# Scan stage of a Mamba, MoE and latent-attention kernel issued in its written order, with loads by their use and the first half's experts and feed-forwards in one queue

## The chip, the cores and the metric

The kernel runs on one core of a Trainium2 chip. The metric is the device time of one launch in microseconds. Three runs of the kernel before took 973.04 to 975.01 us, with a median of 973.29 us. Engines are named as in the profile: PE (matrix products), DVE (vector), ACT (scalar), POOL (GpSimd), SP (issues most of the transfers).

## The reference

Four sequences of 512 tokens and 128 channels pass through three blocks with residuals, and the second kind of block is used twice:

```python
x = x + mamba_then_moe(layernorm(x))
x = x + ffn(layernorm(x))
x = x + latent_attention(layernorm(x))
x = x + ffn(layernorm(x))

def mamba_then_moe(x):
    h = rmsnorm(x, rms1_w)
    xi, z = split(h @ in_proj_w, 2)              # 256 channels each
    xi = silu(causal_conv(xi, conv_w) + conv_b)  # 4 taps
    dt, Bm, Cm = split(xi @ x_proj_w)            # 64, 16, 16
    delta = softplus(dt @ dt_proj_w + dt_proj_b)
    A = -exp(A_log)
    for t in tokens:                             # 16 states per channel
        h_t = exp(delta_t * A) * h_t + (delta_t * xi_t) * B_t
        y_t = sum over states of h_t * C_t
    y = (y + D_skip * xi) * silu(z)
    h = x + y @ out_proj_w
    m = rmsnorm(h, rms2_w)
    top2 of softmax(m @ router_w) over 8 experts
    return h + sum over top2 of weight * (silu(m @ Wg[e]) * (m @ Wu[e])) @ Wd[e]

def latent_attention(x):                         # 16 heads of 8, 64 latents
    q_lat = per head (x @ W_dq.T @ W_uq.T) @ k_eff
    c_kv = x @ W_dkv.T
    return causal softmax(q_lat @ c_kv.T / sqrt(8)) @ c_kv @ v_eff

def ffn(x):                                      # integer weights times 1/127
    return (silu(x @ wg.T) * (x @ wu.T)) @ wd.T
```

## The kernel before

All 512 tokens of a sequence lie on the free axis during the scan: channels are two halves of 128 partitions, so that a tile is 128 x 1024. One state of one sequence is a *step*; there are 4 x 16 = 64 steps, counted by s, in the loop at L733. A step (`scan`, L635) issues:

- `decay(s+2)`, L607: ACT makes the decays da of two steps later, and SP loads the row of C, cs, over all partitions.
- bx, L646: DVE multiplies delta times xi (du) with the row of B that `spread` (L618) put over the partitions with a PE product, pb.
- hst, L650: DVE's scan along the tokens.
- hc, L655: POOL multiplies with cs.
- `accumulate`, L626: PE adds the hc of the step before into PSUM (yp).

Beside these the loop advances generators, a piece at each step. `front(b+1)` (L519) makes the projections, the convolution and delta of the next sequence. `close(b-1)` (L664) ends the one before: y, output projection, RMS norm, router logits, `route` (L698, top two) and `number` (L226, rows of the tokens in the list sorted by expert). `scatter` (L263) writes the tokens to their rows in DRAM, with indirect transfers on POOL. At step 7 of the third sequence `experts(0)` (L326) and two `combine` (L381) are put into the queue `work`, of which a step issues one piece. The sequences form two groups, [0, 1] and [2, 3], and `experts(g)` runs 23 tiles of 128 rows for a group, each tile with three weight loads of 256 KB on SP; tile i's transpose, tile i-1's gate and up products with tanh, and tile i-2's halving (L321) and down product stand in one piece. `plan(g)` (L276) tells which expert and which rows a tile has. `combine` gathers each token's two expert rows with indirect transfers on POOL.

The order of instructions on each engine in this stage is the scheduler's, which starts from the order in which the pieces are written.

Ahead of the loop come the moments of all four sequences (L477 on, `moments` L158, `rsqrt` L142), the integer weights (L499), the zeroing of the two sorted lists xg as two transfers of 4 MB, and three small products that make w_up and veff.

The last stage (L761 on) is the attention with both feed-forwards. `project(b)` (L824) makes queries and keys, each as a sum of three bf16 parts (`three`, L815), and stores them (q_d, k_d) to DRAM; `fill(u)` (L864) loads them for a unit of 8 heads. `maxima(u)` (L875) finds each row's maximum, which goes back to the queries as three more rows through DRAM (m_d). `exps(G)` (L920) makes the exponentials for 4 heads (st on PE, p on ACT), `weigh(G)` (L953) the weighted sums and `divide(G)` (L969) the quotient. Units 0 to 7 run in the loop at L1045, which also steps the queue with `experts(1)`, `combine(2)`, `first_ffn(2)`, `project(2)` and so on to `last(b)`, the second feed-forward of a sequence.

Of the kernel before, what the change touches and what calls it, by code (L numbers as in the profile page):

```python
# [28 lines left out]
WBUFS = 3  # L29
PBUFS = 12  # L30
GROUPS = [[0, 1], [2, 3]]
BIG = 3.0e38


@with_exitstack
def block_kernel(ctx, tc, x, rms1_w, rms2_w, in_proj_w, conv_w, conv_b, x_proj_w,
# [8 lines left out]
    xs = []  # L45
    for b in range(B):
        xt = keep.tile([P, NT, C], F32, tag="x", name=f"x{b}")
        nc.sync.dma_start(xt, x[b].rearrange("(t p) c -> p t c", p=P))
        xs.append(xt)
# [8 lines left out]

    r1w = load("r1w", [P, 1, 1], column(rms1_w, 1), nc.scalar)
    w_in = load("w_in", [P, 2 * EI], in_proj_w, nc.scalar)  # L60
# [4 lines left out]
    A = load("A", [P, NE, NS], A_log.rearrange("(c p) n -> p c n", p=P), nc.scalar)  # L65
    Dk = load("Dk", [P, NE, 1], column(D_skip, NE), nc.scalar)
    w_op = load("w_op", [P, NE, C], out_proj_w.rearrange("(c p) m -> p c m", p=P))
    r2w = load("r2w", [P, 1, 1], column(rms2_w, 1))
    w_rt = load("w_rt", [P, NEXP], router_w)
    w_qk = const.tile([P, 2 * KVL], F32, tag="w_qk", name="w_qk")  # L70
    nc.sync.dma_start(w_qk[:, 0:KVL], W_dqT)
    nc.sync.dma_start(w_qk[:, KVL : 2 * KVL], W_dkvT)
    w_dq = load("w_dq", [KVL, C], W_dq)
    w_uq = load("w_uq", [KVL, C], W_uqT)
    w_uk = load("w_uk", [P, KVL], W_uk)
    w_uv = load("w_uv", [P, KVL], W_uv)
    w_o = load("w_o", [P, C], W_oT)
# [64 lines left out]
    def rsqrt(v, n, pool=small, tag="rs"):  # L142

        r = pool.tile([P, n], F32, tag=f"{tag}{n}", name="rs_r")
# [23 lines left out]
    def layernorm(dst, src):  # L168
        mv = moments(src)
        v = small.tile([P, NT], F32, tag="v", name="ln_v")  # L170
        nc.vector.tensor_scalar(v, mv[:, :, 1], EPS, None, ALU.add)
        r = rsqrt(v, NT)
        for t in range(NT):
            nc.vector.tensor_scalar(
                dst[:, t, :], src[:, t, :], mv[:, t, 0:1], r[:, t : t + 1], ALU.subtract, ALU.mult
            )

# [9 lines left out]
    def transposed(ps, dst, src, scale=None):  # L187

        pt = ps.tile([P, L], F32, tag="mm", name="pt")
        for t in range(NT):  # L190
            nc.tensor.transpose(pt[:, t * P : (t + 1) * P], src[:, t, :], ident)
        if scale is None:
            nc.scalar.copy(dst, pt)
        else:
            nc.scalar.activation(dst, pt, AF.Copy, scale=scale)

    hs = [keep.tile([P, NT, C], F32, tag="hs", name=f"hs{b}") for b in range(B)]
# [18 lines left out]
    ps = ctx.enter_context(tc.tile_pool(name="ps_m", bufs=1, space=PSUM))  # L216
# [9 lines left out]
    def number(b):  # L226
# [12 lines left out]
        nc.vector.tensor_copy(tot, pr[:, 1].rearrange("p j e -> p e j"))  # L239
# [14 lines left out]
        nc.vector.tensor_tensor(row, inc.rearrange("p e j -> p j e"), pr[:, 0], ALU.add)  # L254
# [71 lines left out]
    def experts(g):  # L326
# [4 lines left out]
        xT, wgu, wd, hidden = {}, {}, {}, {}  # L331
        for i in range(NTILES + 2):
            if i < NTILES:
                e = nc.sync.value_load(both[0:1, 0, i : i + 1], min_val=0, max_val=NEXP - 1)
                at = nc.sync.value_load(
                    both[0:1, 1, i : i + 1], min_val=0, max_val=NEXP * ROWS - P
                )
                xt = wt.tile([P, C], F32, tag="xt", name="xt", bufs=3)
                nc.sync.dma_start(xt, sorted_x[g][bass.ds(at, P), :])
# [3 lines left out]
                wd[i] = wt.tile([P, NFC, C], F32, tag="wd", name="wd", bufs=WBUFS)  # L343
# [3 lines left out]
            if i >= 2:  # L347
# [3 lines left out]
            if i < NTILES:  # L351
                pt = ps.tile([P, P], F32, tag="mm", name="mpt")
                nc.tensor.transpose(pt, xt, ident)
                xT[i] = wt.tile([P, P], F32, tag="xTm", name="xTm", bufs=3)
                nc.scalar.activation(xT[i], pt, AF.Copy, scale=r2w[:, 0, :])  # L355
            if 1 <= i <= NTILES:
                x, w = xT.pop(i - 1), wgu.pop(i - 1)
                pgu = []
                for k in range(2):
                    pp = ps_s.tile([P, NFC, P], F32, tag="sc", name=("mpg", "mpu")[k])  # L360
                    for f in range(NFC):
                        nc.tensor.matmul(  # L362
                            pp[:, f, :], w[:, k, f * P : (f + 1) * P], x, start=True, stop=True
                        )
                    pgu.append(pp)
                th = wt.tile([P, NFC, P], F32, tag="thm", name="thm")
                nc.scalar.activation(th, pgu[0], AF.Tanh, scale=0.5)  # L367
                hidden[i - 1] = th, *pgu
            if i >= 2:
# [6 lines left out]
                y = wt.tile([P, C], F32, tag="ym", name="ym")  # L376
                nc.scalar.copy(y, pd)
                nc.sync.dma_start(sorted_y[g][(i - 2) * P : (i - 1) * P, :], y)
            yield

    def combine(b):  # L381

        g = place[b][0]
        for t in range(NT):
            for k in range(2):
# [4 lines left out]
                )  # L390
                nc.vector.scalar_tensor_tensor(
                    base[b][:, t, :], yk, gates[b][:, t, k : k + 1], base[b][:, t, :],
                    ALU.mult, ALU.add,
                )
                yield
# [22 lines left out]
    by_head = w_up.rearrange("p (d h) -> p h d", h=NH)  # L418
    nc.vector.tensor_copy(by_head[0:KVL], w_uq.rearrange("p (h d) -> p h d", d=HS))
    pk = ps.tile([P, L], F32, tag="mm", name="pk")  # L420
    nc.tensor.matmul(pk[:, 0:C], w_uq, w_dq, start=True, stop=True)
# [704 lines left out]
```

## Time and profile before

The profiled execution took 975.5 us, and its span on the core is 973.8 us (1.7 us lie around it).

| Engine | busy us | share of the span | instructions |
|---|---|---|---|
| PE, products | 747.4 | 77% | 3588 |
| DVE | 625.7 | 64% | 1266 |
| ACT | 332.7 | 34% | 576 |
| POOL | 272.7 | 28% | 190 |

| Mark in the trace | us from the span's start |
|---|---|
| first hst | 58.2 |
| first hst of sequences 1, 2, 3 | 128.5, 225.2, 323.1 |
| last hst ends | 445.4 |
| first softmax tile (st) | 572.4 |
| ffn(2) transposes start | 710.8 |
| end | 973.8 |

Transfers moved 92.69 MB, a mean of 95 GB/s. A busy PE in the table is not PE at its peak, since the clock that the chip grants (PEclk in the page) stands at 0.853 in the mean. The span is divided by the marks into a part in which DVE has the most to do (the scan), a part in which neither DVE nor PE is full, and a part in which PE is.

### The profile page before, as it was taken

The page shows a single profiled execution, that of the slowest core. Times are in us where ns is not written, and L with a number is a line of the kernel's source. Part 1 is how long each engine was busy: PE and PEld are TensorE (multiplying, and loading weights), DVE is VectorE, ACT ScalarE, POOL GpSimd, SP SyncE. Part 2 cuts the span into 40 slices and gives each one's busy share as a digit, 9 for nine tenths or more (in the row PEclk, how much of TensorE's full clock was granted, in tenths as well). Part 3 has the DMA queues.
Part 4 walks back from the last instruction along what each step waited for, and adds up shares of the span by engine and source line. Part 5 has one row for each costly group of instructions (what it writes and reads, how often), then busy time and mean ns, then how long its engine had stood idle before and what let it go on. Part 6 is the DMA issues. An engine that isn't in the chain of part 4 may idle for free.

```text
span 973.8 us, 11231 instructions
## 1 busy us (share of the span) xinstructions
PE 747.4 (77%) x3588; PEld 407.9 (42%) x3588; DVE 625.7 (64%) x1266; ACT 332.7 (34%) x576; POOL 272.7 (28%) x190
## 2 busy tenths in 40 slices
PE   0878567766687976787266899979478999999894
PEld 0322222323234743575123366866333445444342
DVE  6279899789988899744754655542257475655523
ACT  0477322352236422321011044324311454433440
POOL 2046664476456443613620000000320010000000
PEclk9989796887699988989577589989776899989898
DMA  8612121111115752563146063855400342100000
GB/s 255 235 48 73 43 65 54 44 44 54 55 48 173 218 159 81 156 205 103 44 122 162 18 166 88 242 176 158 112 20 30 87 116 63 39 13 14 3 11 11
DMA packets 81084, 92.69 MB, mean 95 GB/s; under 512 B 9441, under 2 KB 56489, under 8 KB 79849
## 3 DMA queue, kind: packets, MB, share of 16 engines
q1 hardware_dynamic: 77105, 86.81, 30.2%
q0 software_dynamic: 2048, 4.20, 1.5%
q10 hardware_dynamic: 1872, 0.97, 0.4%
q8 instruction: 28, 0.46, 0.2%
q14 instruction: 31, 0.25, 0.1%
HBM read 70.71 MB, written 21.17 MB: 94 GB/s over the span
## 4 chain that ended last, share of the span: by engine, by line
PE 46%; DVE 27%; issue 11%; DMA 7%; ACT 5%; POOL 2%; SPq 1%; ACTq 0%; POOLq 0%; DVEq 0%
DVE hst L650 9%; PE po L960 6%; DVE bx L646 5%; PE yp L631 4%; PE sc L886 4%; PE st L937 4%; PE mpd L373 3%; PE pg L783 3%; DMA xt<-xg 3%; PE mpu L362 3%; PE mpg L362 2%; DVE mx L895 2%; PE fpd L792 2%; DMA yk<-yg,rows_y 2%; PE pm L538 2%
## 5 line engine op out<-in xcount | busy, mean ns | idle before, releaser
L631 PE MATMUL yp<-hc,ident 128*128 128x512 f32 x256 | 165.9, 755 | 69.0 <-POOL hc L655 66.8
L655 POOL TENSOR_TENSOR hc<-hst,cs 128x1024 f32<-128x1024 f32 x64 | 151.2, 2362 | 159.3 <-DVE hst L650 31.4
L650 DVE TENSOR_TENSOR_SCAN hst<-da,bx 128x1024 f32<-128x1024 f32 x64 | 145.9, 2280 | 2.8
L895 DVE TENSOR_REDUCE mx<-sc 128x1 f32<-128x512 f32 (+3 forms) x176 | 109.1, 638 | 43.0 <-PE sc L890 40.8
L611 ACT ACTIVATE da<-delta,A 128x512 f32<-128x512 f32 (+1 forms) x128 | 86.0, 713 | 141.4 <-DVE hst L650 103.1
L950 ACT ACTIVATE p<-st 128x512 f32<-128x512 f32 x160 | 90.9, 597 | 102.7 <-PE st L945 101.3
L631 PEld LDWEIGHTS yp<-hc,ident 128*128 128x128 f32 x256 | 53.6, 229 | 145.3 <-POOL hc L655 109.7
L646 DVE TENSOR_TENSOR bx<-du,pb 128x1024 f32<-128x1024 f32 x64 | 78.5, 1226 | 28.3 <-PE pb L621 24.0
L886 PE MATMUL sc<-ks,qs 72*128 72x128 bf16 (+3 forms) x256 | 71.4, 339 | 9.4 <-DVE mx L895 7.9
L960 PE MATMUL po<-p,va 128*32 128x512 f32 (+3 forms) x512 | 76.3, 447 | 0.0
L323 DVE SCALAR_TENSOR_TENSOR thm<-thm,mpg 128x512 f32<-128x512 f32 x46 | 31.4, 684 | 67.4 <-ACT thm L367 67.4
L387 POOL DMA_INDIRECT yk<-yg,rows_y x32 | 30.4, 950 | 138.5 <-DMA ks<-k_d 128.1
L937 PE MATMUL st<-qs,ks 75*128 75x512 bf16 (+3 forms) x256 | 63.8, 313 | 1.3 <-ACT p L950 0.9
L373 PE MATMUL mpd<-wd,mh 128*128 128x128 f32 x368 | 55.0, 296 | 2.7 <-ACT xTm L355 1.9
L362 PE MATMUL mpu<-xTm,wgu 128*128 128x128 f32 x368 | 53.6, 288 | 3.6 <-DVE mh L324 1.9
L373 PEld LDWEIGHTS mpd<-wd,mh 128*128 128x128 f32 x368 | 49.4, 206 | 13.9 <-ACT xTm L355 9.4
L986 POOL TENSOR_TENSOR base<-x,yn 128x512 f32<-128x512 f32 x4 | 5.1, 1267 | 177.4 <-DVE yn L981 177.4
L362 PE MATMUL mpg<-xTm,wgu 128*128 128x128 f32 x368 | 54.1, 290 | 0.6 <-DVE thm L323 0.6
L362 PEld LDWEIGHTS mpg<-xTm,wgu 128*128 128x128 f32 x368 | 50.4, 207 | 4.1 <-DVE thm L323 1.7
L362 PEld LDWEIGHTS mpu<-xTm,wgu 128*128 128x128 f32 x368 | 48.9, 204 | 7.3 <-DVE mh L324 4.5
L890 PE MATMUL sc<-maskq,identb 128*128 128x128 bf16 (+2 forms) x176 | 48.1, 273 | 0.0
L886 PEld LDWEIGHTS <-qs 72*128 72x128 bf16 x256 | 25.6, 109 | 42.0 <-issue 35.4
(229 smaller groups left out, 1079.9 us busy)
## 6 DMA issues: line engine op xcount, KB each, us to landing
cs<-c_d SPq DMA_DIRECT2D x64, 256.0 KB
wgu<-in_Wg_dram SPq DMA_DIRECT2D x46, 256.0 KB
wgu<-in_Wu_dram SPq DMA_DIRECT2D x46, 256.0 KB
wd<-in_Wd_dram SPq DMA_DIRECT2D x46, 256.0 KB
xg<-zero SPq DMA_DIRECT2D x2, 4096.0 KB
k_d<-parts SPq DMA_DIRECT2D x12, 384.0 KB
qs<-q_d SPq DMA_DIRECT2D x24, 192.0 KB
ks<-k_d SPq DMA_DIRECT2D x24, 192.0 KB
```

The lines of the kernel that those rows point to most:

```text
L362: nc.tensor.matmul(pp[:, f, :], w[:, k, f * P : (f + 1) * P], x, start=True, stop=True)
L373: nc.tensor.matmul(pd, hT[:, f, :], w[:, f, :], start=(f == 0), stop=(f == NFC - 1))
L611: nc.scalar.activation(da[:, e, e:], delta[b][:, e, e:], AF.Exp, scale=A[:, e, n : n + 1])
L631: nc.tensor.matmul(yps[b][:, e, :], ident, hc[:, e, :], start=(n == 0), stop=(n == NS - 1))
L646: nc.vector.tensor_tensor(bx, du[b], pb.unsqueeze(1).to_broadcast([P, NE, L]), ALU.mult)
L650: nc.vector.tensor_tensor_scan(hst.rearrange("p e l -> p (e l)"), dec.pop(s).rearrange("p e l -> p (e l)"), bx.rearrange("p e l -> p (e l) ...
L655: nc.gpsimd.tensor_tensor(hc, hst, cs.unsqueeze(1).to_broadcast([P, NE, L]), ALU.mult)
L886: nc.tensor.matmul(sc[:, c : c + w], q[0:NP9, h, t * P : w], k[0:NP9, h, 0:w], start=(h == h0), stop=False, skip_group_check=True,)
L895: nc.vector.tensor_reduce(mx[:, t, h0 : h0 + n], sc[:, 0 : n * w].rearrange("p (h k) -> p h k", k=w), AX.X, ALU.max,)
L937: nc.tensor.matmul(pt[:, c : c + L - kt * P], k[0 : NP9 + 3, h0 + j, rows], q[0 : NP9 + 3, h0 + j, kt * P : L], start=(c == 0), stop=False ...
L950: nc.scalar.activation(p, pt, AF.Exp, scale=scale)
L960: nc.tensor.matmul(po[32 * j : 32 * j + 32, kt * P : L], vs[b % 2][:, kt, (4 * g + j) * (HS + 1) : (4 * g + j) * (HS + 1) + 32], got[j][kt ...
```

## The change

The lines are numbered here as in the changed kernel. It does the following.

- **Order.** Everything from the moments of x0 to the last scatter is issued inside `tc.manual_schedule(engines=ORDERED)`: PE, DVE, ACT and SP keep the order in which the code is written. POOL stays with the scheduler, but `queued` ties what is written for it between two steps' products hc to that place, with dependences that carry no wait. The attention stage is left to the scheduler, and its pools take `reuse_waits="tile"`.
- **Start.** x0 and the weights of `front(0)` are loaded first, and moments and deviations are made for x0 alone. `early()` makes the others, the zeroing (8 transfers of 1 MB), the integer weights and `prepare()` (w_up, veff, constants of the values), a piece at each step of the first sequence.
- **Steps.** `front` and `close` have more and smaller pieces; `close` begins at step 1 and not 0, `scatter` at 6 and not 4 with two a step, `experts(0)` at 9 and not 7. In the last sequence every second step takes two pieces of `work`. Copies of logits, counts and of the output projection are on ACT, the sum h2 on POOL.
- **Experts.** Rows are loaded a tile ahead, results stored a tile later, and buffers of the gate and up weights are 2 and not 3.
- **Feed-forward.** `ffn` moves to the common part; its xn, xT and fh have one buffer each, shared with `project`; the end is a copy on ACT and a sum on POOL. `first_ffn(0)` and `first_ffn(1)` follow `combine(0)` and `combine(1)` in the queue, which is emptied before `project(0)`.
- **Attention.** `project`'s parts are split on POOL, which also issues the stores of q_d and k_d and both transfers of m_d. `maxima` issues a tile's reduce behind the next tile's products; `weigh` holds the quotient too; the evacuations of mT, values and quotients are on ACT. The queue is stepped by a rate (0.8, 0.7, 0.4 a piece).

```diff
-WBUFS = 3
+WBUFS = 2
+ORDERED = {ENG.PE, ENG.DVE, ENG.Activation, ENG.SP}
...
+        def early():
+            for b in range(1, B):
+                moments(xs[b], mv0[:, b])
+            yield
+            deviations(range(1, B))
+            yield
+            zero = w1.tile([P, NE * L], F32, tag="y", name="zero")
+            nc.gpsimd.memset(zero, 0.0)
...
+            yield from prepare()
...
+        order = mybir.DependencyInfo(mybir.DependencyClass.NoSync, mybir.DependencyReason.DATA)
+        mark = []
+        def queued(ins):
+            traced = nc.cur_bb.bb.instructions
+            if mark:
+                at = next(k for k in reversed(range(len(traced))) if traced[k] is mark[0])
+                between = [i for i in traced[at + 1 :] if i.engine == ENG.Pool and i is not ins]
+                for i in between:
+                    tc.add_manual_dep(i, mark[0].name, order, reason="behind the step's product")
+                for i in between or mark:
+                    tc.add_manual_dep(ins, i.name, order, reason="before the step's product")
+            mark[:] = [ins]
...
-            h2 = w2.tile([P, NT, C], F32, tag="h2", name="h2")
-            nc.vector.tensor_tensor(h2, h0[b], po, ALU.add)
+            h2 = w1.tile([P, NT, C], F32, tag="h2", name="h2")
+            nc.scalar.copy(h2, po)
+            nc.gpsimd.tensor_tensor(h2, h0[b], h2, ALU.add)
+            yield
...
+        with tc.manual_schedule(engines=ORDERED):
+            moments(xs[0], mv0[:, 0])
+            deviations([0])
...
                 for n in range(NS):
                     scan(b * NS + n)
-                if n == 0 and b:
-                    behind = close(b - 1)
-                next(behind, None)
-                if n == 4 and b:
+                    if n >= 1:
+                        next(behind, None)
+                    if n == 6 and b:
                         rows_out.add(scatter(b - 1))
-                rows_out.step(3)
+                    rows_out.step(2)
                     if n >= 2:
                         next(ahead, None)
-                if n == 7 and b and place[b - 1][1] == len(GROUPS[0]) - 1:
+                    if n == 9 and b and place[b - 1][1] == len(GROUPS[0]) - 1:
                         g = place[b - 1][0]
                         work.add(experts(g), *(combine(i) for i in GROUPS[g]))
-                work.step()
+                        work.add(*(first_ffn(i) for i in GROUPS[g]))
+                    next(rest, None)
+                    work.step(2 if b == B - 1 and n % 2 else 1)
+        with tc.manual_schedule(engines=ORDERED):
+            accumulate(*late.pop(0))
+            for _ in close(B - 1):
+                work.step()
+            for _ in scatter(B - 1):
+                work.step(n % 2)
+                n += 1
...
+                nc.scalar.copy(parts[:, 0, :], pq)
+                nc.scalar.copy(full, pq)
+                nc.gpsimd.tensor_tensor(full, full, parts[:, 0, :], ALU.subtract)
+                nc.gpsimd.tensor_copy(parts[:, 1, :], full)
+                nc.gpsimd.tensor_tensor(parts[:, 2, :], full, parts[:, 1, :], ALU.subtract)
+                if half == 0:
+                    nc.gpsimd.dma_start(q_d.rearrange("j d h l -> (d h) j l"), parts)
...
-        work.add(first_ffn(0), project(0))
         work.empty()
+        run(project(0), steps(work, 0))
         fill(0)
         fill(1)
-        work.add(first_ffn(1), project(1), experts(1), combine(2), first_ffn(2), project(2))
-        work.add(combine(3), first_ffn(3))
-        run(times(3, maxima(0)), steps(work, 12))
+        work.add(experts(1), combine(2), first_ffn(2), project(2))
+        work.add(combine(3), first_ffn(3), project(3))
+        run(chain(project(1)), steps(work, 6))
+        run(times(2, maxima(0)), steps(work, 6))
```

## The prediction

> **What bounds the kernel now.** I read the page's slices first, then the chain that ended last, the busy time by stage, and two stretches of the timeline. The slices (40 of 24.3 us) show which engine is full where:
>
> ```profile
> PE 0878567766687976787266899979478999999894
> DVE  6279899789988899744754655542257475655523
> PEclk9989796887699988989577589989776899989898
> ```
>
> DVE is at eight to nine tenths from slice 5 to 18, the scan; PE from slice 30 on, the attention. Between them (slices 19 to 23) neither is full.
>
> ```profile
> PE 46%; DVE 27%; issue 11%; DMA 7%; ACT 5%; POOL 2%; SPq 1%; ACTq 0%; POOLq 0%; DVEq 0%
> ```
>
> The chain says the same: PE and DVE in turn, 18% issue and DMA. The table by stage has for each window busy time and count of PE, PEld, DVE, ACT and POOL, then PE's clock, DMA share and GB/s. Its windows are the second, third and fourth sequence of the scan, the way from the last scan to the first softmax tile, a hole, and the rest:
>
> ```profile
> 128.50:225.20 96.70, 67.48 (x146) 26.65 (x147) 82.34 (x101) 36.38 (x52) 57.03 (x31) 0.83 0.16 49
> 225.20:323.10 97.90, 74.67 (x236) 36.67 (x236) 87.48 (x127) 40.39 (x63) 55.45 (x30) 0.85 0.31 93
> 323.10:445.40 122.30, 99.12 (x545) 71.23 (x544) 94.30 (x123) 38.37 (x81) 46.98 (x26) 0.89 0.55 166
> 445.40:572.40 127.00, 80.07 (x313) 46.14 (x311) 68.78 (x250) 15.20 (x30) 33.69 (x31) 0.65 0.30 83
> 694.00:711.00 17.00, 0.17 (x2) 0.17 (x1) 7.86 (x35) 0.64 (x2) 11.81 (x14) 0.52 0.28 64
> 711.00:973.80 262.80, 234.78 (x1370) 113.51 (x1370) 142.51 (x396) 93.32 (x166) 11.48 (x10) 0.89 0.14 37
> ```
>
> DVE has little idle time in the second and third, more in the fourth, where the expert tiles run. The fourth row is serial work at clock 0.65; the fifth is an empty PE; the last is PE-bound (89%). An undisturbed step of the scan, and one with routing in it:
>
> ```profile
> 74.31 2.29 DVE L650 TENSOR_TENSOR_SCAN hst<-da,bx 128x1024 f32<-128x1024 f32 x1
> 76.71 1.23 DVE L646 TENSOR_TENSOR bx<-du,pb 128x1024 f32<-128x1024 f32 x1
> 78.07 2.29 DVE L650 TENSOR_TENSOR_SCAN hst<-da,bx 128x1024 f32<-128x1024 f32 x1
> ...
> 276.96 2.34 POOL L655 TENSOR_TENSOR hc<-hst,cs 128x1024 f32<-128x1024 f32 x1 [2.48 <-issue]
> 277.17 2.19 DVE L723 TENSOR_TENSOR hits<-key,first 128x32 f32<-128x32 f32 x1
> 280.50 0.19 DVE L723 TENSOR_TENSOR hits<-key,first 128x32 f32<-128x32 f32 x1
> ```
>
> Start to start the step is 78.07 - 74.31 = 3.76 us, and 16 make 60. The two L723 lines are the same operation: 0.19 us alone, 2.19 us when it starts 0.21 us into POOL's product hc and ends with it. In this order most small operations stand alone between bx and hst and take 1 us each (0.98 to 1.26 us at 244 to 264, where the step is 4.7 us). bx, hst and the halvings of an expert tile (L323, L324), which read a PSUM operand, keep their durations beside hc.
>
> **Part 1, the start.** Only x0's moments and deviations now stand ahead of front(0). Before, hn starts at 23.67 us. After: x0 is there at 4.4, moments 1.2 us, then some 30 operations of 4 columns at 0.2 us with a few casts and the w_k products (4 x 0.6), so about 13.8. From hn to the first hst (34.5 us in before: 23.67 to 58.16) nothing is changed but the PSUM pool. First hst at 48.3: **-10** (-7 if the conv weights' load, now on SP's queue behind x0, is late; -12).
>
> **Part 2, the scan.** The written order on DVE gathers small operations behind hst: in the built kernel's order 8, 8, 11 and 15 of the 16 steps of the four sequences have anything but bx and hst, and 6, 6, 7 and 3 have operations with SBUF operands alone. Those start against hc. Price of such a step: 2.2 us as at 277.17 (2.19), or 1.0 us as at 244 to 264, if the first operation slips in ahead of hc. I take 2.2, since one step holds many operations and the second meets hc. The rest are free durations from rows of before. That work is added to 60 us:
> - Sequence 0: lock 6 x 2.2 = 13; moments of x1 to x3 3.7; deviations 27 x 0.2 = 5.4; front(1) on DVE hn and h 2.5, rest and mid 1.1, d and two delta sums 3.2; weights and copies 1.3. Sum 90 (before 70.4): +20. This is where the start's saving goes: the moments are not saved but moved.
> - Sequence 1: lock 13; front 6.8; close: y 1.4, rmsnorm 3.7, route and number 26 x 0.2 = 5.2. 90 (before 96.7): -7.
> - Sequence 2: lock 15; the same 17; plan 5; three tiles x 2 x 0.68 = 4; waiting for PE and tables 2. 103 (before 97.9): +5.
> - Sequence 3: lock 7; close 10; 20 tiles x 1.36 = 27; seven steps take two tiles, and the second's halving waits on DVE for that tile's gate and up products (0.9 + 0.9 us) issued in the same step, 1.6 us each = 11, with bx and hst queued behind it. 115 (before 122.3, of which DVE waited 18.3 us for tanh): -7.
>
> POOL gets zeroing of 'zero', the h2 sums (1.27 us each) and scatters (0.95 + 0.3 us, two a step) between products; it is busy 47 to 57 of about 97 us, which hides them, and without that cover a scatter step costs 2 x 1.25 = 2.5 us, 4 steps a sequence. SP gets the zeroing as 8 x 1 MB in place of 2 x 4 MB; DMA share is 0.16 to 0.31 there. cs with three buffers in place of four, hc two to three, weights three to two: costed at nothing, hidden if a tile's three loads (0.79 MB, 3.6 us at the 218 GB/s of the fullest slice there) fit into its step: 5.1 us with one tile, 8.1 with two. That is thin; if it goes, PE waits for weights as it did for xt in the fourth sequence (7.7 us).
>
> Scan sum: 20 - 7 + 5 - 7 = +11, with the start **+1**: the last hst ends at 446. Bounds: with 1.0 us for each of 22 locked steps -26; with 8 scatter steps uncovered and late weights +28.
>
> The Trainium skill, page "SBUF — State Buffer", section "Who interferes with whom", says that VectorE and GpSimd share a port pair, that an operation with two SBUF inputs, or in a two-port mode, blocks for the whole of a GpSimd operation that holds it, and that the order of issue decides who waits. The 2.19 us row agrees. Taken whole, 2.35 us for 22 steps would make 52 us of locks against 48 in my sum, and it speaks against gathering small operations behind hst, where hc starts; but before they already met it in more steps.
>
> **Part 3, to the attention.** Before, the last hst is followed by close(3) (y 453.7, po 457.6, h2 460), eight gathers a sequence with their sums to 482, ffn(0) 482 to 497, project(0) to 517, ffn(1) and project(1) to 542, maxima(0) to 558, first softmax tile 572.4: 127 us, with 1.8 tiles of experts(1) done. After, combine(0) is mostly done inside the scan. But ffn(0), ffn(1), project(0) share the buffers xn, xT and fh and run one after another: 15 + 18 us for the two, then project(0) 20 us with its splitting in three POOL operations per half (1.15 to 1.27 us) and its loads on POOL's queue. POOL's scatter of sequence 3 and the ffn sums stand ahead of these; fill(0) waits on them, and SP's loads for the tiles behind it. Adding from the last hst, T: gathers of combine(1) stand on POOL ahead of y, so close ends at T+37; its number and plan and combine(1)'s sums stand on DVE ahead of ffn(0), which begins at T+48; ffn(1) done T+83, k_d landed T+107, maxima(0) T+126, then the tiles and maxima(1) written ahead of the first softmax: T+154. **+27** (+10 if the scheduler, free in this stage, slips project between; +35).
>
> What that time buys: 9.6 tiles done by then in place of 1.8. In before the tiles between 596 and 664 take 3.9 us each, so 7.8 x 3.9: **-30** (0 to -38).
>
> **Part 4, the hole and the end.** PE stood empty at 694 to 711:
>
> ```profile
> 710.84 1.24 PE L191 MATMUL pt<-ident,xn 128*128 128x128 f32 x4 [16.83 <-DVE xn L174]
> ```
>
> ffn(2)'s transposes wait for combine(2)'s gathers, and softmax work is queued behind. With experts(1) done earlier those gathers lie beside the second unit's exponentials: **-17** (0 if the rates bring tiles and transposes together again). PE ran 33.8 of the 55 us after 690 at 0.70; at 0.9, as in the last window, that is 7.5 less; ACT copy and POOL sum at the last ffn in place of one DVE sum cost +1.3 (0.6 + 1.27 - 0.69, rounded): **-6** (0 to -10). Maxima's later reduce, weigh with divide, mT on ACT: costed at nothing beside PE at 89%; without that cover an ACT copy is 0.6 us.
>
> **Sum.** 1 + 27 - 30 - 17 - 6 = -25 on the profiled execution's 975.5 (span 973.8 and 1.7 around it), 950. Its median over the runs is 973.3, 2.2 less: **948**.
>
> **Rivals.**
> A, slower. The tiles are not ahead at the first softmax. Their loads are on SP behind the fills, these behind k_d, this behind POOL's parts; DMA waits of 7 us for xt in the last sequence speak for it, the nearly free queues (DMA share 0.30) against. The +27 stays and the -30 goes: 948 + 30 = 978. It decides when fewer than 1.8 + (30 - 25) / 3.9 = 3 tiles are done at the first softmax.
> B, no net change. Rates make PE wait for combine(2) or (3) again and the clock stays low: 948 + 17 + 6 = 971. For it: PE is in order and the same gathers stand before ffn(2). Against: nothing else waits there.
> C, a larger gain. Small operations slip ahead of hc at 1.0 us, and the serial part runs in +10: 948 - 26 - 17 = 905; half of it 926. For it: hc starts some 0.05 to 0.2 us behind hst; against: the 2.19 us row.
> That the order does nothing is out for DVE: the built order differs at each of the steps counted above.
>
> **Numbers.** Forecast (930 to 966) 0.49, C 0.20, A 0.23, B 0.08. The measurement tells 0.2% (2 us) from no change, so of B half is within that. Faster 0.49 + 0.20 + 0.02 = 0.71, same 0.04, slower 0.25. Range: C's full price at the bottom, A with the uncovered scatters (8 x 2.5 = 20, half of it) at the top, 905 to 988. The forecast's own is 930 to 966.
>
> **What would show it.** First hst near 48; steps of 3.76 us where nothing stands between, and 6 where routing does; 90, 90, 103, 115 us a sequence; last hst near 446; first softmax near 600 with nine or ten mpd groups of the second plan ahead of it; no PE gap over 5 us after it. A last hst beyond 460, or a first softmax beyond 610 with few tiles done, makes the forecast wrong.

## The result, and the profile after

The changed kernel is slower. Its median is 983.32 us over 11 runs (977.82 to 989.85) against 968.85 for the kernel before over 11 runs; the ratio is 1.0141, with a 95% interval of 1.0100 to 1.0182. The forecast was 948, a gain of 2.6%. The profiled execution took 983.32 us and its span is 981.6, against 973.8 before.

The slices of the page after the change (40 of 24.5 us), for PE, DVE and PE's granted clock:

```profile
PE   3439666756684976886246889798898989999974
DVE  4299899889989967777554175335365365655621
PEclk9758887978796988998567579799996979999997
```

DVE is fuller in the first slices of the scan (nine tenths in slice 2, seven before) and as full as before up to slice 13. The low stretch of PE between scan and attention lies around slices 19 to 21. The chain that ended last can't be set beside that of before: its shares add up to about 13%, so it is followed back only a short way.

```profile
PE 9%; DVE 1%; issue 1%; ACT 1%; DMA 1%; POOLq 0%; POOL 0%; DVEq 0%; ACTq 0%
```

So the reading goes by stages, with the same marks as before: the second, third and fourth sequence, the way from the last hst to the first softmax tile, and the rest (columns: busy time and count of PE, PEld, DVE, ACT, POOL, then PE's clock, DMA share and GB/s).

```profile
136.50:230.90 94.40, 62.35 (x150) 25.78 (x149) 84.14 (x99) 40.96 (x61) 58.48 (x34) 0.85 0.17 51
230.90:332.50 101.60, 71.72 (x225) 36.30 (x225) 93.02 (x128) 41.97 (x66) 57.98 (x32) 0.82 0.27 82
332.50:455.00 122.50, 100.89 (x607) 79.09 (x606) 95.95 (x124) 43.21 (x93) 49.13 (x27) 0.93 0.58 179
455.00:622.70 167.70, 107.49 (x492) 68.03 (x491) 84.11 (x264) 27.98 (x60) 51.55 (x51) 0.69 0.40 113
622.70:981.60 358.90, 317.69 (x1968) 167.16 (x1967) 172.36 (x466) 151.37 (x283) 53.51 (x60) 0.91 0.23 63
```

Set against the marks of before and the forecast's terms, all from the two profiled executions:

| stage | before | after | moved | forecast |
|---|---|---|---|---|
| to the first hst | 58.2 | 47.6 | -10.5 | -10 |
| sequence 0 | 70.4 | 88.8 | +18.4 | +20 |
| sequence 1 | 96.7 | 94.4 | -2.3 | -7 |
| sequence 2 | 97.9 | 101.6 | +3.7 | +5 |
| sequence 3, to the last hst's end | 122.3 | 122.5 | +0.2 | -7 |
| to the first softmax tile | 127.1 | 167.7 | +40.6 | +27 |
| to the end | 401.4 | 358.9 | -42.5 | -53 (-30 - 17 - 6) |
| sum | 973.8 | 981.6 | +7.8 | -25 |

Every term has the sign that was forecast but sequence 3's; four sizes are off, all to the slower side: sequences 1 and 3 by 5 and 7 us, the way to the first softmax by 14, the rest by 10. The way to the first softmax is the largest of them.

### The profile page after: what moved, and what is told of

Its sections match the earlier page's. It is cut to its first block, busy times and chain, and to the rows that moved or that the text cites. A ratio compares the mean times of both kernels' runs of the same rounds, so it can differ in the third digit from the quotient of the medians.

```text
span 981.6 us, 11382 instructions
## 1 busy us (share of the span) xinstructions
PE 737.6 (75%) x3588; PEld 406.2 (41%) x3588; DVE 627.0 (64%) x1242; ACT 362.2 (37%) x641; POOL 324.5 (33%) x250
## 5 line engine op out<-in xcount | busy, mean ns | idle before, releaser
L728 POOL TENSOR_TENSOR hc<-hst,cs 128x1024 f32<-128x1024 f32 x64 | 151.3, 2364 | 174.7 <-DVE hst L723 66.2
L689 PE MATMUL yp<-hc,ident 128*128 128x512 f32 x256 | 147.0, 703 | 22.7 <-POOL hc L728 14.0
L964 DVE TENSOR_REDUCE mx<-sc 128x1 f32<-128x384 f32 (+3 forms) x168 | 103.3, 636 | 75.6 <-PE sc L972 74.5
L1046 PE MATMUL po<-p,va 128*32 128x384 f32 (+3 forms) x512 | 86.3, 451 | 0.0
L679 PE MATMUL pb<-bc,pick 96*128 96x512 bf16 x64 | 27.6, 431 | 71.5 <-DVE bx L719 70.0
L1021 PE MATMUL st<-qs,ks 75*128 75x512 bf16 (+3 forms) x256 | 65.0, 326 | 10.9 <-DMA qs<-m_d 10.4
L968 PE MATMUL sc<-ks,qs 72*128 72x128 bf16 (+3 forms) x256 | 68.1, 324 | 6.2 <-DVE mx L964 4.9
L997 POOL DMA_DIRECT2D m_d<-mT x8 | 4.4, 550 | 195.3 <-ACT mT L995 195.3
L348 PE MATMUL mpg<-xTm,wgu 128*128 128x128 f32 x368 | 56.7, 301 | 12.3 <-DMA wgu<-in_Wg_dram 6.0
L360 PE MATMUL mpd<-wd,mh 128*128 128x128 f32 x368 | 50.3, 279 | 1.1 <-ACT xTm L341 0.6
L360 PEld LDWEIGHTS mpd<-wd,mh 128*128 128x128 f32 x368 | 45.9, 195 | 2.8 <-ACT xTm L341 1.7
L354 ACT ACTIVATE thm<-mpg 128x512 f32<-128x512 f32 x46 | 27.5, 597 | 46.4 <-PE mpg L348 45.7
```

What stands on the lines that cost most here:

```text
L348: nc.tensor.matmul(pp[:, f, :], w[:, k, f * P : (f + 1) * P], rows_in, start=True, stop=True,)
L360: nc.tensor.matmul(pd, hT[:, f, :], w[:, f, :], start=(f == 0), stop=(f == NFC - 1))
L689: nc.tensor.matmul(yps[b][:, e, :], ident, hc[:, e, :], start=(n == 0), stop=(n == NS - 1))
L728: queued(nc.gpsimd.tensor_tensor(hc, hst, cs.unsqueeze(1).to_broadcast([P, NE, L]), ALU.mult).ins)
L964: nc.vector.tensor_reduce(*taken, AX.X, ALU.max)
L968: nc.tensor.matmul(sc[:, c : c + w], q[0:NP9, h, t * P : w], k[0:NP9, h, 0:w], start=(h == h0), stop=False, skip_group_check=True,)
```

## The experiments

Each experiment was timed beside runs of the kernel before, whose median moved between 967 and 973 us, so ratios to that median are compared and not times. Stage times are read from one profiled execution of each kernel. Comments in the code cuts (`# ...`) say what a cut stands for. First the stages were exchanged whole.

**e1: the scan stage of the change, the attention stage of before.**

```diff
-    with ExitStack() as second:  # the changed kernel's attention stage
+    work.empty()
+    with ExitStack() as fourth:  # the one of before, with its ffn and layernorm
...
-                        work.add(*(first_ffn(i) for i in GROUPS[g]))
```

> The changed kernel's scan stage with the attention stage of before (its project, ffn, maxima, weigh, divide and queue). The traces put the last hst's end 9.6 us later than before and the way from there to the end 1.8 us shorter. Theory: the loss is made in the scan stage, so this kernel ends its scan near 455 us as the changed one does and takes 127 + 401 us from there: 983 to 986, slower than before by 8 to 12. Rival: the attention stage has lost time and the scan's end is paid back by the experts and combine sums that it has already done: then this kernel is faster than the changed one by 10 or more, near 970.

Measured: 999.44, ratio 1.0321 (1.0290 to 1.0352); last hst's end 454.7, first softmax 140.1 later (before 127.1), then 404 to the end.

**e2: the scan stage of before, the attention stage of the change.**

```diff
-    with ExitStack() as fourth:
+    with ExitStack() as second:  # the changed kernel's, ffn in its own pools
+        work.add(first_ffn(0), first_ffn(1))
...
```

> The scan stage of before with the attention stage of the change; the feed-forwards 0 and 1 run ahead of project(0) as there. Theory (loss in the scan): last hst's end near 445, then about 527 us, so 971 to 975, no slower than before. Rival (loss in the attention stage, two serial feed-forwards ahead of project(0)): 980 to 990, first softmax tile 165 us or more after the last hst.

Measured: 930.63, ratio 0.9604 (0.9568 to 0.9640). Its two stages after the scan:

```profile
442.90:599.70 156.80, 111.65 (x562) 73.38 (x561) 84.45 (x275) 29.32 (x62) 50.53 (x51) 0.75 0.46 130
599.70:932.60 332.90, 296.85 (x1947) 159.09 (x1946) 170.94 (x462) 150.01 (x282) 53.60 (x60) 0.96 0.24 65
```

In both runs the theory (the loss lies in the scan) had the direction right and the size far too small. The attention stage alone gains 4.0% and the scan stage alone loses 3.2%. Added up that would be a gain of 0.8%, but together they lose 1.4%, so 2.2% lies in how they fit together. After the first softmax this kernel needs 332.9 us where the changed one needs 358.9, with the same attention code. What differs there is the queue: experts and combine of before, and the buffers. e8, e10 and e11 take this up. First the written order.

**e3: the scan stage in the scheduler's order.**

```diff
-        with tc.manual_schedule(engines=ORDERED):
+        with ExitStack():
```

> The changed kernel without the written order in the scan stage: the scheduler may move instructions on PE, DVE, ACT and SP; all else stays. Theory: the written order costs time because small operations stand in one lump behind hst and a tile's halving waits for PE; given free, the sequences take less, above all the fourth (122.5 us, steps of 19 and 12 us): last hst's end near 445 and 973 to 978 in all. Rival: the order is worth having (the forecast's -7 in the sequences 1 and 3) and the scheduler does worse: scan end at 460 or later, 985 to 1000.

Measured: 962.99, ratio 0.9959 (0.9929 to 0.9989), from 953.73 to 969.08 in ten runs, of which the fastest was profiled. Sequence 0 takes 66.1 us in place of 88.8, the first softmax comes 154.1 after the last hst in place of 167.7. Sequences 1 to 3 take 100.7, 103.4 and 124.9 (94.4, 101.6 and 122.5 in the written order), though the theory named the fourth as the place of the loss. So the written order costs at both ends of the stage and gains some 10 us in sequences 1 to 3.

**e4: a step's small work between bx and hst.**

```diff
+            between()      # close, front, early, scatter, queue
             hst = w3.tile([P, NE, L], F32, tag="hst", name="hst", bufs=2)
```

> The changed kernel with a step's small work written between bx and hst in place of behind hst, so that the first operation with two SBUF operands meets the last 1.0 us of the hc of the step before and not the first 2.35 us of the step's own. Theory of the port: 19 blocked operations took 33.7 us over their free duration; each loses up to 1.2 us less, so the scan ends up to 20 us earlier and the kernel takes 963 to 975. Rival: what stands in the steps is work and waits for PE, POOL and ACT, and putting it ahead of hst only delays hst and hc: 980 to 990.

Measured: 992.90, ratio 1.0268 (1.0196 to 1.0340). The sequences take 79.4, 93.3, 104.8 and 141.5 us. An operation of DVE that runs beside one of POOL and takes longer than the shortest of its shape is called blocked here. The excess of blocked operations fell from 43 us to 26, and sequence 0 gained 9.4 us; but with the queue's tiles ahead of hst, bx waits 28.6 us for PE's pb in the fourth sequence, where the changed kernel has no such wait, and that sequence lost 19 us. The two were mixed in one edit; e14 takes them apart.

**e5 and e6: the written order without PE, and without DVE.**

```diff
-ORDERED = {ENG.PE, ENG.DVE, ENG.Activation, ENG.SP}
+ORDERED = {ENG.DVE, ENG.Activation, ENG.SP}   # e5
+ORDERED = {ENG.PE, ENG.Activation, ENG.SP}    # e6
```

> The changed kernel with the written order kept on DVE, ACT and SP and left to the scheduler on PE. Theory that PE's written order is what costs (in the fourth sequence and after the last hst, PE waits at the transposes of hs and at po with ready tile products queued behind): most of the 29.6 us between the spans of the changed kernel and of the free one comes back, scan end near 447, 955 to 965. Rival, DVE's order (small operations behind hst, combine's sums ahead of y): little moves, 978 to 988.

> The written order kept on PE, ACT and SP, DVE left to the scheduler. Theory that DVE's order is what costs: first sequence 68 us in place of 88.8 as in the free kernel (66.1), scan end near 445, first softmax 154 us after it, 955 to 965. Rival, PE's order: first sequence shorter but the fourth stays at 120 us or more, 970 to 985.

Measured: e5 991.60 (1.0251, 1.0195 to 1.0307), e6 951.04 (0.9839, 0.9779 to 0.9898). PE's written order is worth having: without it the fourth sequence takes 131.4 us in place of 122.5. DVE's is what costs: without it sequence 0 takes 71.8 us, the scan ends at 437.1 and the first softmax follows 154.6 later. Sequences 1 and 2 stay (94.4 and 102.0).

**e9: the moments of x1 to x3 behind front(0)'s hn.** What e6's scheduler did with sequence 0 can be written by hand.

```diff
             first = front(0)
             next(first)
+            for b in range(1, B):
+                moments(xs[b], mv0[:, b])
+            deviations(range(1, B))
```

(and they are taken out of `early`)

> The changed kernel, written order kept; the moments and deviations of x1 to x3 are written behind front(0)'s hn, where DVE waits for ACT and PE, and no longer behind the scans of steps 0 and 1. Theory: the start's saving was given back in the first sequence because these 10 us of DVE work were moved from a place with room (DVE idle 17 us before the first sequence in the kernel before) into one without. First hst stays at 47 to 48.5, the first sequence falls from 88.8 to 78, and the time by 8 to 11 us, 972 to 976. Rival: the first hst moves later by what the sequence gains, no change, 981 to 985.

Measured: 971.21 (1.0046, 1.0020 to 1.0072): 9 us less than the changed kernel by the ratios, 12 by the medians, in one edit. The timeline of DVE in the changed kernel, from its wait in `front(0)` to step 2 (in brackets the idle time and its releaser):

```profile
32.59 0.69 DVE L636 TENSOR_TENSOR bc_rest<-pbc,bc 96x512 f32<-96x512 f32 x1 [16.31 <-ACT bc_c L632]
47.64 2.29 DVE L723 TENSOR_TENSOR_SCAN hst<-da,bx 128x1024 f32<-128x1024 f32 x1
54.27 2.29 DVE L723 TENSOR_TENSOR_SCAN hst<-da,bx 128x1024 f32<-128x1024 f32 x1
65.42 2.29 DVE L723 TENSOR_TENSOR_SCAN hst<-da,bx 128x1024 f32<-128x1024 f32 x1
```

And in e9:

```profile
33.12 0.69 DVE L630 TENSOR_TENSOR bc_rest<-pbc,bc 96x512 f32<-96x512 f32 x1 [7.86 <-ACT bc_c L626]
48.18 2.29 DVE L717 TENSOR_TENSOR_SCAN hst<-da,bx 128x1024 f32<-128x1024 f32 x1
50.57 1.23 DVE L713 TENSOR_TENSOR bx<-du,pb 128x1024 f32<-128x1024 f32 x1
51.91 2.29 DVE L717 TENSOR_TENSOR_SCAN hst<-da,bx 128x1024 f32<-128x1024 f32 x1
```

The first hst is only 0.5 us later than in the changed kernel (47.64), and steps 0 and 1 take 3.7 us each where they took 6.6 and 11.1. Sequence 0 falls to 78.5. In the changed kernel DVE stood idle for 16.3 us until ACT's bc_c was there; with the moved work in that place 7.9 us of the idle time are left.

**e7: what follows the last step left to the scheduler.**

```diff
-        with tc.manual_schedule(engines=ORDERED):
+        with ExitStack():
             accumulate(*late.pop(0))
             for _ in close(B - 1):
```

> The changed kernel with only what is written after the last step (last close, its scatter and the queue's pieces beside them) left to the scheduler. Theory: combine's sums, which wait for gathers on DVE's queue ahead of y, delay the last close; the way from the last hst to the first transposes of ffn(0) falls from 47.4 to 36 us as in the free kernel and the time by 8 to 12 us, 971 to 975; scan end stays at 455. Rival, POOL's gathers ahead of y set it: 980 to 985.

Measured: 965.59 (0.9968, 0.9938 to 0.9997), 17 us less than the changed kernel by the ratios, where 8 to 12 were expected. From the last hst's end to ffn(0)'s transposes it takes 35.3 us in place of 47.4. The profiled execution was the slowest of its ten, and it places only these 12 us. The mechanism is in POOL's queue. The changed kernel's timeline of POOL shows the gathers of combine(1) (yk) and the scatter's rows (xg):

```profile
473.47 0.97 POOL L375 DMA_INDIRECT yk<-yg,rows_y  x1 [0.16 <-issue]
474.46 1.27 POOL L761 TENSOR_TENSOR base<-x,h 128x512 f32<-128x512 f32 x1
486.56 0.96 POOL L375 DMA_INDIRECT yk<-yg,rows_y  x1 [10.84 <-DVE base L381]
487.83 0.95 POOL L375 DMA_INDIRECT yk<-yg,rows_y  x1 [0.30 <-DVE crow L235]
```

A gather needs one of four yk buffers, and these come free when DVE has added them. Those sums stand, as written, behind rmsnorm and routing of the last sequence on DVE, so POOL waits 10.8 us, and ffn(0) waits for the sums. POOL's waits in e7, from 456 to 505:

```profile
POOL xg L249 <- DVE cmove L270: 11.6, 1, 11.6
POOL yk L375 <- issue: 2.8, 10, 0.3
POOL xg L249 <- issue: 2.1, 7, 0.3
POOL yk L375 <- DVE base L381: 0.6, 3, 0.3
```

The wait has gone from the gathers (0.6 us) to the scatter (11.6 us), for whose rows nothing is in a hurry. The rival (POOL's gathers ahead of y) falls: y's product still starts 9.7 us after the last hst's end here, as it did. That it is DVE's order and not PE's shows in e5 and e6: with PE free the wait is 10.9 us and the way to ffn(0) 47.4, with DVE free 0.6 and 35.2.

**e8, e10 and e11: the stretch after the first softmax.** All three are e3 with two buffers for xn, xT and fh in the attention stage (e11: one for fh). e10 has the combine of before, e11 its experts and three weight buffers.

```diff
+        xn = w2.tile([P, NT, C], F32, tag="xn", name="axn", bufs=2)   # e8, e10, e11: xT and ffn's too
...
         for t in range(NT):                                            # e10: combine as before
             for k in range(2):
                 yk = wt.tile([P, C], F32, tag="yk", name="yk", bufs=4)
...
                 yield                                                  # eight pieces, not five
...
+WBUFS = 3                                                              # e11, hc two buffers
```

> The free kernel (scheduler's order in the scan) with two buffers for xn, xT and fh of feed-forward and projection in the attention stage in place of one. From the first softmax tile to the end the free kernel takes 353 us, the one with the scan of before and two buffers 333. Theory: the shared single buffers put projections and feed-forwards one behind the other; two bring 15 to 20 us, 333 to 340 us, 940 to 948. Rival: it is the third weight buffer that is missing, and these change nothing: 353, 960.

> The free kernel with two buffers (e8: 955, from the first softmax tile to the end 349 us) with the combine of before: one gather and its sum a piece, eight pieces in place of five. In e2, with the queue's pieces of before, that stretch took 333 us. Theory: the queue's pacing is the difference; eight pieces put ffn(2) later beside more of the softmax: 333 to 341 us, 940 to 947. Rival: it is the experts' pieces and the third weight buffer: 349, 952 to 958.

> The free kernel with two buffers for xn and xT and the experts of before (rows loaded with the weights, result stored at once, three buffers of the gate and up weights; hc back to two buffers to make room). Theory of the third buffer and the pieces: from the first softmax tile to the end 333 to 341 us, 940 to 947. Rival (combine's pieces): 349 us, 952 to 960, and a slower fourth sequence if hc's two buffers bind.

Measured: e8 954.96 (0.9897, 0.9832 to 0.9961), e10 934.37 (0.9655, 0.9611 to 0.9700), e11 952.55 (0.9849, 0.9814 to 0.9883). By the medians e10 is 21 us faster than e8; the profiled executions, e8's fastest and e10's slowest, show 9 of them. Before the first softmax e8 and e10 agree within 2 us. From there to the end, e8 first, e10 second:

```profile
595.80:945.00 349.20, 309.98 (x1968) 164.80 (x1967) 173.42 (x466) 150.81 (x283) 53.62 (x60) 0.93 0.23 65
```

```profile
597.60:936.00 338.40, 301.66 (x1968) 162.97 (x1967) 175.63 (x466) 151.29 (x283) 53.61 (x60) 0.94 0.23 65
```

The same number of PE instructions, 10.8 us apart: 8.3 of them are PE's busy time. Nothing but combine differs: it is handed out in eight pieces and not five, and a gather's sum stands in the gather's own piece and not in the next one. Which of the two counts was not taken apart. Two buffers bring 4 us of this stretch (353.3 in e3), a third weight buffer with the experts of before none (350.5 in e11). e2's 332.9 is not reached here, but e12 below reaches 331.9 with the experts and the combine of before together: what the experts of before bring shows only with combine in eight.

**e12: all of it at once.** DVE free as in e6, two buffers for xn and xT, experts and combine of before, three weight buffers.

> DVE left to the scheduler in the scan (e6: 951, scan end 437.1), two buffers for xn and xT, experts and combine of before with three weight buffers. If the gains add: scan end 437 to 440, then 490 us as in e2, 925 to 932, faster than e2 (930.6) or level with it. If the fourth sequence loses by one tile's load no longer ahead: 935 to 940.

Measured: 989.36 (1.0253, 1.0209 to 1.0298). The gains do not add: the fourth sequence takes 178.2 us. e15 below has the same order of engines with the changed kernel's experts, and 122.4. The experts of before load a tile's rows in the piece that transposes them and store its result at once, and here PE and SP keep to that order. In e12 PE's largest wait in the fourth sequence is for those rows; the second line is the same wait in e15 (us in total, times, longest):

```profile
PE mpt L334 <- DMA xt<-xg: 49.7, 17, 4.0
PE mpt L339 <- DMA xt<-xg: 2.0, 3, 0.8
```

SP stands 94.3 us behind results (ym) there, 35.4 in e15. e12 also has two buffers of hc, but no wait of DVE for hc shows in this sequence.

**e13 and e14: the written order, mended.** e13 joins e9, e7 and e10 in the changed kernel; e14 also moves the small work between bx and hst, as e4, but leaves the queue's tiles behind hst.

```diff
+            between()                # e14: close, front, early, scatter
...
                     scan(b * NS + n, between)
+                    work.step(2 if b == B - 1 and n % 2 else 1)
```

> The changed kernel in its written order with three places mended: moments and deviations of x1 to x3 behind front(0)'s hn (e9), what follows the last step left to the scheduler (e7), combine in eight pieces with two buffers for xn, xT and fh in the attention stage (e10). Theory that these three are the cause: scan end 445 as in e9, first softmax 153 to 156 us later, 338 us from there: 936 to 940, that is 3% faster than before where the forecast said 2.6%. Rival (the gains do not add, PE's or DVE's order costs elsewhere): 950 or more.

> As e13, with the small work of a step (close, front, weights, scatter) written between bx and hst and the queue's tiles left behind hst. In e4 the blocked time fell from 42 to 26 us but the tiles ahead of hst cost 19 us in the fourth sequence. Theory of the port: sequences 1 and 2 gain up to 5 us each over e13, 926 to 934. Rival: sequences as in e13 or longer, because what is moved ahead of hst waits for ACT or POOL and hst and hc wait behind it: 936 to 945.

Measured: e13 947.03 (0.9746, 0.9689 to 0.9804), e14 932.74 (0.9581, 0.9531 to 0.9631). With three places mended the written order gives 2.5%, near the 2.6% that was forecast for it unmended. It missed its own 936 to 940. Combine's eight pieces reach into the fourth sequence (129.5 us, of which 5.2 in one wait for a gather), but the 6 us by which the scan ends late come back on the way to the first softmax (148.4 for 153 to 156); what stays is the last stretch, 343.6 for 338. e14 is 1.5% faster than e13. How a blocked operation looks, in the timeline of DVE, first the changed kernel's (routing behind hst), then e14's (numbering between bx and hst):

```profile
165.36 0.19 DVE L793 TENSOR_REDUCE best<-lg 128x4 f32<-128x32 f32 x1
165.58 2.28 DVE L794 TENSOR_TENSOR ez<-lg,best 128x32 f32<-128x32 f32 x1
167.78 0.18 DVE L799 TENSOR_TENSOR key<-lg,best 128x32 f32<-128x32 f32 x1
```

```profile
159.55 1.30 DVE L222 TENSOR_TENSOR_SCAN cinc<-restart,ctot 128x32 f32<-128x32 f32 x1
160.88 0.17 DVE L229 TENSOR_TENSOR cend<-region,cinc 128x8 f32<-128x8 f32 x1
161.09 0.19 DVE L230 TENSOR_TENSOR cinc<-cinc,ctot 128x32 f32<-128x32 f32 x1
```

One operation of such a group takes until the product hc ends (POOL's hc ran from 165.46 to 167.81 and from 158.40 to 160.76), 2.28 us or 1.30, and the others are as short as alone. Other sums of POOL do the same: in e14 an operation of the RMS norm takes 1.11 us beside base. The excess of blocked operations fell from about 40 us in e13 to about 22 in e14. But the sequences 1 and 2, for which the theory gave 5 us each, stayed (94.7 to 93.9, 101.6 to 101.9); sequences 0 and 3 gained 3.7 and 7.5. So e14's time came within the theory's range by another road than the theory's. In sequence 1 the time went into a wait of bx for pb of 5.2 us, PE being behind the transposes of hs.

**e15: DVE free, combine in eight, two buffers.**

```diff
-ORDERED = {ENG.PE, ENG.DVE, ENG.Activation, ENG.SP}
+ORDERED = {ENG.PE, ENG.Activation, ENG.SP}
...
+        xn = w2.tile([P, NT, C], F32, tag="xn", name="axn", bufs=2)
```

> DVE left to the scheduler in the scan (e6, scan end 437.1, first softmax 154.6 us later) with combine in eight pieces and two buffers (338 us to the end): 437 + 153 + 338 = 928, 925 to 932 and so level with e2. Rival: combine in eight pieces stretches the queue into the last close: 936 to 942.

Measured: 935.05 (0.9630, 0.9569 to 0.9690), between the theory's range and the rival's; scan end 438.1, first softmax 151.3 later, then 343.0 to the end for the 338 of e10.

| kernel | ratio to before | last hst's end | to first softmax | to the end |
|---|---|---|---|---|
| before | 1 | 445.4 | 127.1 | 401.4 |
| changed | 1.0141 | 455.0 | 167.7 | 358.9 |
| e2, attention stage alone | 0.9604 | 442.9 | 156.9 | 332.9 |
| e6, DVE free | 0.9839 | 437.1 | 154.6 | 355.9 |
| e10, free order, combine in eight | 0.9655 | 445.0 | 152.6 | 338.4 |
| e13, written order mended | 0.9746 | 451.2 | 148.4 | 343.6 |
| e14, small work ahead of hst too | 0.9581 | 440.4 | 148.0 | 343.3 |

e14, e2, e15 and e10 are the fastest, and their intervals overlap.

## Why the prediction was wrong

**Part 1** held, step by step: hn starts at 13.5 us for 13.8, and from there the first hst takes 34.1 us for 34.5. **Part 2** was right where it priced locks and moved work. The excess of blocked operations in the four sequences is 10, 13, 14 and 6 us, against 13, 13, 15 and 7 in the sum; sequences 0 and 2 came out within 2 us; and the forecast's sentence that the moments are moved and not saved was the truth of sequence 0. It left one thing out that the trace of before showed (DVE idle 17.4 us ahead of the first sequence): there was a place where they cost little. e9 shows it, 10.2 us of sequence 0. Sequences 1 and 3 were mis-sized. In sequence 1 DVE waits for ACT and POOL inside front:

```profile
196.41 0.69 DVE L636 TENSOR_TENSOR bc_rest<-pbc,bc 96x512 f32<-96x512 f32 x1 [3.22 <-ACT bc_c L632]
210.01 3.35 DVE L658 TENSOR_TENSOR delta<-delta,sp_d 128x1024 f32<-128x1024 f32 x1 [2.93 <-POOL sp_d L656]
```

The 3.22 and 2.93 us in brackets were in no term. In sequence 3 the term for the second tile's halving was 11 us; DVE waited 20.4 us for tanh. That freeing DVE leaves these two sequences at 94.4 and 120.3 (e6) says that they were sized too low, not that DVE's written order is at fault there. No run takes these waits away, so this part of the account is argued.

**Part 3** is the step that failed: first softmax at T+167.7 for T+154, where T is the last hst's end. Its marks held up to maxima(0): ffn(0) began at T+47.4 for T+48, ffn(1) was done at T+81.1 for T+83, the last reduce of maxima(0) ended at T+126.3 for T+126. The term that failed is the last one, 28 us for the tiles and maxima(1) ahead of the first softmax. It took 41.4 us:

```profile
580.65 0.69 DVE L981 TENSOR_REDUCE mx<-sc 128x1 f32<-128x512 f32 x1
608.50 0.38 PE L991 MATMUL pmx<-identb,mparts 128*24 128x128 bf16 x4
609.79 0.57 POOL L997 DMA_DIRECT2D m_d<-mT  x1 [41.67 <-ACT mT L995]
616.32 0.52 POOL L998 DMA_DIRECT2D qs<-m_d  x1 [5.96 <-DMA m_d<-mT]
617.78 0.22 PE L972 MATMUL sc<-maskq,identb 128*128 128x128 bf16 x1
622.68 0.58 PE L1021 MATMUL st<-qs,ks 75*128 75x512 bf16 x1 [4.68 <-DMA qs<-m_d]
```

For 36.7 us PE works on eight tiles, maxima(1) and the values (busy 33.8 at a clock of 0.95, so this is work and not waiting). By the forecast's own price of 3.9 us the eight tiles alone would have made 31: it booked them as a gain behind the first softmax at more than it paid for them ahead of it. Then PE stands 4.7 us for the maxima of unit 0. Their transposes (pmx) come 27 us after the last reduce, behind seven of the tiles, and their way through DRAM to the first softmax takes 14.2 us, which had no term. In the kernel before pmx follows 0.9 us after the reduces, and the way through DRAM, 14.9 us, lies beside other work of PE:

```profile
556.67 0.18 DVE L817 CAST mparts<-mx 128x32 bf16<-128x32 f32 x1
557.58 0.60 PE L907 MATMUL pmx<-identb,mparts 128*24 128x128 bf16 x4 [1.67 <-DVE mparts L820]
572.43 0.39 PE L937 MATMUL st<-qs,ks 75*128 75x512 bf16 x1
```

Every run with the changed attention stage has this: 26 to 29 us from the reduces to pmx and 13 to 14 from there to the softmax, whatever the order in the scan. e1, with the stage of before, has 0.9 and 15.1. No run moves pmx alone, so why the scheduler puts it there, and what an earlier pmx would bring, stay open.

What e7 mends is another thing. Its 12 us lay inside the T+48, which the forecast had reached for a reason that did not hold: it put the gathers on POOL ahead of y, but y's product starts 9.75 us after the last hst's end, 9.8 in the kernel before. The delay came from the loop between gathers and sums that e7 opens. That T+48 was met is luck, and the loop is a loss that the changed kernel need not have.

**Part 4** had its mechanism right. Nine tiles' down products ran ahead of the first softmax, as forecast, and the empty PE of 16.8 us ahead of ffn(2) is gone: after the first softmax PE has no gap over 5 us until the last feed-forward. The size was off, -42.5 for -53. PE's busy time fell by 28.9 us where the tiles and the clock were to bring 37.5, its idle time by 13.6. Between e8 and e10 the same stretch differs by 10.8 us through combine, and e13 and e14, in the written order with combine in eight, need 343.6 and 343.3 us for it where e9 and e7 need 355.7 and 358.5. The forecast had no term for how the queue hands out combine.

**Readings.** Two readings of the forecast were off, neither by much. DVE is at seven and four tenths in slices 16 to 18, not eight to nine. And 3.9 us is the mean of the first eleven tiles after 596; all of them up to 664 take 4.4.

**The rivals.** A (tiles not ahead) did not happen, though the time came near to its 978; the slower side was reached by another road. B (PE waits for combine again) did not happen either. Of C neither half did in the changed kernel: the serial part took +40.6 for its +10, and most blocked operations behind hst took the full 2.2 us. e14 has the cheaper locks and e2 the 4% of the attention stage, both with a serial part of 148 us or more. The lock, which carried C and the range, is not what separates the kernels: its excess is 37 us before and 43 after.

## What to carry to other kernels

Work that is moved ahead of a point has to be paid there at the price at which it is saved behind it. For each transfer on the path, look where its producer stands in its engine's order: the row maxima here waited 27 us for their transposes. Before moving work off a start-up path, look for the engine's idle time on that path: work moved into a stage that the same engine bounds was paid in full here (10.2 us in e9). Where an order is written by hand, follow each buffer of a pool to the instruction that frees it, and see what stands ahead of that instruction on its own engine; a loop through two engines' lists is not seen in either list alone. A stage that loses can hide one that gains: exchange whole stages first, then the parts.

## What the runs showed that had not been expected

The written order of one engine can be worth having while that of another costs: PE's brought 8 to 11 us (e5), DVE's cost 29 to 32 (e6), by medians and by ratios. And PE's busy time for the same 1968 products and transposes was 301.7 us in e10 and 317.7 in the changed kernel, at a granted clock of 0.94 and 0.91. The clock differs by 3% and the busy time by 5%, so the clock is not all of it; that the pacing of the queue sets the clock was not shown.
